# Output projection in steps of two heads, loads three steps ahead, six places per attention tile

## The chip, the core and the metric

The kernel runs on one core of one Trainium2 chip. Its time is the device time in microseconds; lower is better. TensorE does the matrix products, VectorE and ScalarE the work on elements, GpSimd fills constants, and SyncE issues nearly all DMA transfers. SyncE, like the other engines, works through its instructions in order: an instruction that waits holds up all behind it on that engine.

## What is computed

One decoder layer on two sequences of 512 tokens with 1024 features, in float32: attention with a sliding window of 128 and an output projection, cross products with a quantised context, and a quantised feed forward, each with a residual and a layer norm.

```python
def _L0_attn_ref(x, wq, wk, wv, wo):
    q = (x @ wq.T).reshape(B, N, N_Q, HD).transpose(0, 2, 1, 3)    # 32 heads of 128
    k = (x @ wk.T).reshape(B, N, N_KV, HD).transpose(0, 2, 1, 3)   # 8 heads
    v = (x @ wv.T).reshape(B, N, N_KV, HD).transpose(0, 2, 1, 3)
    o = _gqa_swa_attention(q, k, v, SLIDE)
    o = o.transpose(0, 2, 1, 3).reshape(B, N, N_Q * HD)
    return o @ wo.T
...
x = _layernorm(x + _L0_attn_ref(x, L0_attn_wq, L0_attn_wk, L0_attn_wv, L0_attn_wo), axis=-1)
x = _layernorm(x + _L0_xattn_ref(x, ctx_4096, ...), axis=-1)   # fake_quant(x) @ fake_quant(ctx)
x = _layernorm(x + _L0_ffn_ref(x, L0_ffn_w_gate, L0_ffn_w_up, L0_ffn_w_down), axis=-1)
```

The feed forward is silu(gate) * up with 2752 inner features, rounded to whole numbers, times w_down.

## The kernel before

**Products by Strassen's scheme.** Large products are cut into two by two blocks and done with seven block products instead of eight (`strassen`, L99; its matmuls are L109). The left factors need sums of weight blocks (`strassen_left`, L86, lines L92 to L95 on VectorE). A "piece" is one of the seven: four matmuls of 128x256 in float32, each of which the profile shows as two records.

**Attention** (`attention`, L181) goes over 16 groups, first the eight of sequence 0, then the eight of sequence 1. A group has four query heads and is done in four tiles of 128 tokens. In each tile stand, in program order: the scores (L294) with the softmax on VectorE and ScalarE (L301 to L316), pieces of the next group's projections (taken from `rest`), the transposes `pt` of the softmax's result (L322), its two copies `cur` and `both` (L328, L329), further pieces, and the weighing of the values (`weigh`, L341 and L342). A group has 22 pieces; four tiles of six take them all before the last tile's end, so that the last tile has four. Projection weights come through a pool of two buffers (`load_weight`, L203). At a group's end `keep` stores the attention output and its Strassen sums to a scratch tensor in DRAM (`kept`).

**Places.** At each call of `between` (three in a tile) `in_attention` (L903) lets a step of other work in. Three queues of such work exist. `behind` holds the context's quantisation and then the two output projections, one step a call. `aside` holds the cross products of sequence 0, one step a tile. `ahead` holds the sums of the output weights (`sum_output_weights`, 32 steps) and then of the gate and up weights (`sum_weights`, 42 steps): one step a tile while sequence 0 is in attention, two a tile after.

**Output projection** (`project_out`, L387). It runs one level of Strassen over the 32 heads: two halves `q` of the rows, seven products `k`, four steps `s` each, 56 steps. A step loads the left factor (`ol`, 256 KB) from `kept` and the right factor (`or`, 1024 KB) from the output weights or their sums, and does four matmuls of 128x512 (L434). The loads go one step ahead into two buffers. The projection of sequence 0 runs in the attention of sequence 1; that of sequence 1 starts in the last group, must wait for the last heads' `keep` for its steps with `s == LAST`, and runs on in the feed forward (`feed_forward`, L579), where `in_feed_forward` gives it four of the seven places of a unit.

**Order.** The framework places the instructions of each engine in an order of its own that follows data dependences and an estimate of durations; it is fixed when the kernel is built. So a VectorE operation may stand ahead of its place in the source, and waits there in order.

Of the kernel before, what the change touches and what calls it, by code (L numbers as in the profile page):

```python
# [9 lines left out]
F32 = mybir.dt.float32  # L10
# [8 lines left out]
P = 128  # L19
# [3 lines left out]
D = 1024  # L23
KC = D // P
NTT = NT // P
TPB = N // P
NQ = 32
NKV = 8
# [5 lines left out]
HALF = 512  # L34
KH = KC // 2
# [145 lines left out]
def attention(nc, tc, consts, xbuf, tpool, ps_p, ps_y, dram, kept, complete, between):  # L181
# [5 lines left out]
    with ExitStack() as ctx:  # L187
# [9 lines left out]
        STEPS = 6  # L197
# [3 lines left out]
        weights, lefts, right = {}, {}, {}  # L201
# [164 lines left out]
        for m, (b, g) in enumerate(groups):  # L366
            if m + 1 == NKV:
                x1 = load_x(1)
                right[1] = strassen_right(nc, tpool, x1, "t_1")
            rest = pieces(m + 1) if m + 1 < len(groups) else iter(())  # L370
            for i in range(TPB):
                s = scores(b, g, i)
                for _ in range(4):
                    next(rest, None)
                between(b, g, i)
                cur, both = transpose_p(b, g, i, s)
                between(b, g, i)
                for _ in range(STEPS - 4 if i < TPB - 1 else STEPS * TPB):
                    next(rest, None)
                weigh(b, g, i, cur, both)  # L380
                between(b, g, i)
            keep(b, g)
            if g == NKV - 1:
                complete.add(b)


def project_out(nc, b, xres, spaces, psum, kept, complete, wo_d, sums, x_d):  # L387

    respool, stream, work = spaces
    LAST = NKV // 2 - 1
    steps = [(q, k, s) for q in range(2) for k in (1, 6, 2, 7, 5, 4, 3) for s in range(LAST + 1)]

    steps[:8] = [(0, k, s) for k in (1, 6) for s in range(LAST)] + [(0, k, LAST) for k in (1, 6)]
    loaded = {}

    def load(n):
        if n >= len(steps):
            return  # L400
        q, k, s = steps[n]
        left = stream.tile([P, 2, 2, P], F32, tag="left", name=f"ol_{b}_{n}")
        nc.sync.dma_start(out=left, in_=kept[:, k - 1, ts(s, 2), :, ts(q, P)])
        right = stream.tile([P, 2, 2, HALF], F32, tag="right", name=f"or_{b}_{n}")
        src = wo_d[(0, 2, 3)[k - 1]] if k <= 3 else sums[:, k - 4]
        nc.sync.dma_start(out=right, in_=src[:, ts(s, 2)])
        loaded[n] = left, right

    while b and (b - 1, "tokens") not in complete:
        yield  # L410
    load(0)
    yield
    x = respool.tile([P, TPB, D], F32, tag="xres", name=f"xres{b}")
    for i in range(TPB):
        nc.sync.dma_start(out=x[:, i], in_=x_d[ts(b * TPB + i, P), :])
        xres[b * TPB + i] = x[:, i]
    for n, (q, k, s) in enumerate(steps):
        while n + 1 < len(steps) and steps[n + 1][2] == LAST and b not in complete:
            yield
        load(n + 1)  # L420
        left, right = loaded.pop(n)
        if s == 0:
            if k in (1, 6, 5):
                ps = psum.tile([P, HALF], F32, tag="p", name=f"y_{b}_{n}")
                if k == 1:
                    one = ps
                    p1, u2, u3 = (work.tile([P, HALF], F32, tag=f"y{j}", name=f"y{j}_{b}_{n}") for j in range(3))
                elif k == 6:
                    two = ps
                else:  # L430
                    three = ps
        ps = one if k in (1, 2) else three if k in (5, 3) else two
        for c in range(4):
            nc.tensor.matmul(  # L434
                ps, left[:, c // 2, c % 2], right[:, c // 2, c % 2],
                start=k in (1, 6, 5) and s == 0 and c == 0, stop=s == LAST and c == 3,
                skip_group_check=True,
            )
        if s == LAST:
            c11, c12, c21, c22 = (x[:, 2 * h + q, ts(e, HALF)] for h in range(2) for e in range(2))  # L440
            add = lambda out, in0, in1: nc.vector.tensor_tensor(out, in0, in1, ALU.add)
            if k == 1:
                nc.scalar.copy(p1, one)
            elif k == 6:
                add(u2, two, p1)
            elif k == 2:
                add(c11, one, c11)
            elif k == 7:
                add(u3, two, p1)
            elif k == 5:  # L450
                add(u3, three, u3)
                add(c22, u3, c22)
            elif k == 4:
                add(p1, two, p1)
                add(c21, p1, c21)
            else:
                add(u2, three, u2)
                add(c12, u2, c12)
                complete.add((b, q))
        yield  # L460
# [118 lines left out]
def feed_forward(nc, tc, ident, xres, spill, x2T, tpool, early, gate_up, wd_d, pools, stream, out, between, finish_between):  # L579

    wgu_d = gate_up[0]
    _, raw_pool, b_work, ps_p = pools
    with ExitStack() as ctx:
# [15 lines left out]
        acc, left, raw, halves, acts = {}, {}, {}, {}, {}  # L599
# [86 lines left out]
        def down(us, i, e):  # L686

            b, m = units[us[0]]
            t = b * TPB + i
            ps = ps_d.tile([P, HALF], F32, tag="d", name=f"d_{us[0]}_{i}_{e}")  # L690
            down_parts(ps, us, i, e, True, True)
            if m == 0:
                if e == 0:
                    acc[t] = accp.tile([P, D], F32, tag=f"acc{i}", name=f"acc{t}")
                nc.vector.tensor_copy(acc[t][:, ts(e, HALF)], ps)
            else:
                nc.vector.tensor_tensor(acc[t][:, ts(e, HALF)], ps, acc[t][:, ts(e, HALF)], ALU.add)  # L697
            if us[-1] % PER == NCHUNK and e == 1:
                x = stream.tile([P, 2, 2, HALF], F32, tag="right", name=f"fin_x_{t}").rearrange("p a b c -> p (a b c)")[:, :D]
                nc.sync.dma_start(out=x, in_=spill[t])  # L700
                ends.append((t, x, [acc[t]]))

# [87 lines left out]
def decoder_layer(ctx, tc, x, xT, ctx_kv, wq, wk, wv, wo, s1, z1, s2, z2, wgu, wgu_rest, wd, out):  # L790
    nc = tc.nc
    const = ctx.enter_context(tc.tile_pool(name="const", bufs=1))
    resid = ctx.enter_context(tc.tile_pool(name="resid", bufs=1))
    stream = ctx.enter_context(tc.tile_pool(name="stream", bufs=2))
    y_work = ctx.enter_context(tc.tile_pool(name="y_work", bufs=1))

    ident = const.tile([P, P], F32, tag="ident", name="ident")
# [74 lines left out]
    def sum_weights(pool):  # L872


        steps = [(m, k) for m in range(NCHUNK) for k in range(0, KH, 2)]

        def load(m, k):
            w = pool.tile([P, 2, 2, 2, P], F32, tag="w", name=f"raw_{m}_{k}")
            for h in range(2):
                for j in range(2):  # L880
                    c = j * KH + k
                    nc.sync.dma_start(out=w[:, h, j], in_=wgu[m, :, h, c : c + 2])
            return w

        ahead = load(*steps[0])
        for n, (m, k) in enumerate(steps):
            w = ahead
            if n + 1 < len(steps):
                ahead = load(*steps[n + 1])
            if k == 0:  # L890
                sums.append(scratch.tile([P, 4, KH, P], F32, tag=f"sums{m}", name=f"sums{m}"))
            a11, a12, a21, a22 = (w[:, h, j] for h in range(2) for j in range(2))
            s = pool.tile([P, 3, 2, P], F32, tag="s", name=f"sum_{m}_{k}")
            s1_, s2_, s4_ = (s[:, q] for q in range(3))
            tc.keep_in_program_order(nc.vector.tensor_tensor(s1_, a21, a22, ALU.add))
            nc.vector.tensor_tensor(s2_, s1_, a11, ALU.subtract)
            nc.vector.tensor_tensor(a21, a11, a21, ALU.subtract)
            nc.vector.tensor_tensor(s4_, a12, s2_, ALU.subtract)
            nc.sync.dma_start(out=sums[m][:, 0:3, k : k + 2], in_=s)
            nc.sync.dma_start(out=sums[m][:, 3, k : k + 2], in_=a21)  # L900
            yield

    def in_attention(b, g, i):  # L903
        calls[0] += 1
        if (b, g, i) == (0, 2, 0) and calls[0] % 3 == 1:
            behind.add(cross.context(0), 3)
        if (b, g, i) == (1, 0, 1) and calls[0] % 3 == 1:
            behind.add(output(0, ps_y))
            behind.add(output(1, pools[3]))
            aside.add(cross_tokens(0))  # L910
        behind.step()
        if calls[0] % 3 == 0:
            aside.step()
            if b and g == NKV - 1 and (0, "tokens") in complete and not early:
                prepare_feed_forward()
        if calls[0] % 3 == 0 and (b or g or i):
            ahead.step()
            if b:
                ahead.step()

    early = []

# [18 lines left out]
    def in_feed_forward(k):  # L941
        if k in (1, 5):
            aside.step()
        elif k != 3:
            behind.step()

    def finish_between():
        behind.drain()
# [55 lines left out]
```

## Time and profile before

| | us |
|---|---|
| median of 3 runs | 2029.87 |
| lowest and highest run | 2022.77, 2032.69 |
| the profiled execution | 2027.27 |
| its span, first to last instruction | 2024.8 |
| TensorE busy in it | 1962.9 (97%) |
| VectorE, ScalarE, GpSimd busy | 1185.1, 536.0, 14.2 |
| DMA, mean over the span | 213 GB/s, 430.6 MB |

The span has five parts: start (to about 27 us), the first attention (to about 480), the second attention with the first output projection (to about 1100), the feed forward with the second output projection (to about 1490), and the rest of the feed forward. TensorE's busy time counts a matmul that runs at half clock in full; the share of the clock that was granted stands beside it in the table by stretches. In a timeline, a bracket behind a row gives how long the engine stood idle before it and what ended that. "SPq" is SyncE's queue of DMA issues, and "to landing" is the time from issue to the last byte.

### The profile page before, as it was taken

The page shows a single profiled execution, that of the slowest core. Times are in us where ns is not written, and L with a number is a line of the kernel's source. Part 1 is how long each engine was busy: PE and PEld are TensorE (multiplying, and loading weights), DVE is VectorE, ACT ScalarE, POOL GpSimd, SP SyncE. Part 2 cuts the span into 40 slices and gives each one's busy share as a digit, 9 for nine tenths or more (in the row PEclk, how much of TensorE's full clock was granted, in tenths as well). Part 3 has the DMA queues.
Part 4 walks back from the last instruction along what each step waited for, and adds up shares of the span by engine and source line. Part 5 has one row for each costly group of instructions (what it writes and reads, how often), then busy time and mean ns, then how long its engine had stood idle before and what let it go on. Part 6 is the DMA issues. An engine that isn't in the chain of part 4 may idle for free.

```text
span 2024.8 us, 22067 instructions
## 1 busy us (share of the span) xinstructions
PE 1962.9 (97%) x8022; PEld 1445.1 (71%) x8032; DVE 1185.1 (59%) x2347; ACT 536.0 (26%) x1227; POOL 14.2 (1%) x34
## 2 busy tenths in 40 slices
PE   8999999999999999999999999999999999999995
PEld 6888878887655656666775666666678878888884
DVE  4666766675434355445854453633467688666666
ACT  1223332222111123122433221212133245222225
POOL 0000000000000000000000000000000000000000
PEclk9999999999999999999999999999999999999998
DMA  8355745557878887988537986667743435434421
GB/s 311 128 182 185 238 162 182 181 173 247 293 267 299 299 278 278 305 296 286 181 126 254 343 313 231 237 222 265 255 153 111 138 140 203 165 134 169 149 86 42
DMA packets 220012, 430.60 MB, mean 213 GB/s; under 512 B 16256, under 2 KB 150400, under 8 KB 200192
## 3 DMA queue, kind: packets, MB, share of 16 engines
q1 hardware_dynamic: 218752, 427.10, 60.4%
q10 hardware_dynamic: 1152, 2.10, 0.3%
q8 instruction: 63, 1.03, 0.2%
q14 instruction: 45, 0.37, 0.1%
HBM read 354.68 MB, written 74.45 MB: 212 GB/s over the span
## 4 chain that ended last, share of the span: by engine, by line
PE 79%; DMA 10%; DVE 6%; ACT 2%; issue 1%; SPq 1%; DVEq 0%; ACTq 0%
PE prod L109 43%; PE y L434 16%; PE d L683 8%; PE ps L294 4%; DMA or<-in_wo_dram 3%; DMA or<-wo_sums 3%; PE o L341 2%; DMA w<-in_wq_dram 2%; PE o L342 2%; PE m L551 1%; PE pt L322 1%; DMA xT<-in_xT_dram 1%; PE whole L676 1%; DMA w<-in_wv_dram 0%; DMA kept<-oS 0%
## 5 line engine op out<-in xcount | busy, mean ns | idle before, releaser
L434 PE MATMUL y<-or,ol 128*128 128x512 f32 x896 | 413.1, 604 | 24.0 <-DMA or<-in_wo_dram 12.2
L434 PEld LDWEIGHTS y<-or,ol 128*128 128x128 f32 x896 | 169.9, 193 | 203.9 <-issue 190.9
L109 PE MATMUL prod<-t,wgu 128*128 128x256 f32 x1312 | 302.2, 379 | 0.1
L109 PEld LDWEIGHTS prod<-t,wgu 128*128 128x128 f32 x1312 | 248.5, 190 | 45.4 <-issue 11.2
L109 PE MATMUL prod<-x2T,wgu 128*128 128x256 f32 x984 | 229.8, 379 | 1.0 <-DVE u_None L135 1.0
L109 PEld LDWEIGHTS prod<-x2T,wgu 128*128 128x128 f32 x984 | 186.6, 190 | 38.7 <-issue 12.4
L109 PE MATMUL prod<-xT,w 128*128 128x256 f32 x752 | 180.0, 380 | 1.3 <-ACT st L118 1.3
L109 PE MATMUL prod<-t,s 128*128 128x256 f32 x752 | 175.9, 379 | 0.0
L109 PE MATMUL prod<-t,w 128*128 128x256 f32 x752 | 175.2, 379 | 0.3 <-DVE st L121 0.3
L109 PEld LDWEIGHTS prod<-t,w 128*128 128x128 f32 x752 | 141.8, 190 | 21.9 <-issue 1.6
L109 PEld LDWEIGHTS prod<-t,s 128*128 128x128 f32 x752 | 141.0, 190 | 22.8 <-issue 3.3
L697 DVE TENSOR_TENSOR acc<-d,acc 128x512 f32<-128x512 f32 x152 | 104.7, 691 | 89.3 <-PE d L683 89.1
L109 PEld LDWEIGHTS prod<-xT,w 128*128 128x128 f32 x752 | 139.6, 190 | 24.2 <-issue 5.3
L683 PE MATMUL d<-hi,act 128*128 128x512 f32 x352 | 152.5, 433 | 2.3 <-DVE act L652 2.1
L683 PE MATMUL d<-lo,act 128*128 128x512 f32 x352 | 139.0, 395 | 0.0
L310 ACT ACTIVATE s<-s,top 128x128 f32<-128x128 f32 x256 | 99.7, 391 | 71.3 <-DVE top L307 71.2
L294 PE MATMUL ps<-kT,qT 128*128 128x256 f32 (+1 forms) x512 | 111.5, 353 | 0.0
L294 PEld LDWEIGHTS ps<-kT,qT 128*128 128x128 f32 x512 | 88.5, 190 | 30.7 <-issue 19.2
L302 DVE COPY_PREDICATED s<-mask_i,ps 128x512 f32<-128x512 int32 x64 | 46.7, 730 | 108.0 <-ACT s L301 103.3
L625 ACT CAST hi<-wd 128x1024 fp32r<-128x1024 f32 x44 | 46.0, 1046 | 226.5 <-PE d L683 115.9
L346 ACT COPY oT<-o 128x512 f32<-128x512 f32 x64 | 37.4, 585 | 216.8 <-PE o L342 109.1
L683 PEld LDWEIGHTS d<-hi,act 128*128 128x128 f32 x352 | 66.0, 187 | 39.7 <-DVE acc L697 20.4
(194 smaller groups left out, 2185.1 us busy)
## 6 DMA issues: line engine op xcount, KB each, us to landing
or<-wo_sums SPq DMA_DIRECT2D x64, 1024.0 KB, 6.3
or<-in_wo_dram SPq DMA_DIRECT2D x48, 1024.0 KB, 6.7
wgu<-sums SPq DMA_DIRECT2D x41, 1024.0 KB, 7.3
w<-in_wq_dram SPq DMA_DIRECT2D x64, 512.0 KB, 4.5
ol<-kept SPq DMA_DIRECT2D x112, 256.0 KB, 3.7
raw<-in_wgu_dram SPq DMA_DIRECT2D x168, 128.0 KB, 5.0
wd<-in_wd_dram SPq DMA_DIRECT2D x42, 512.0 KB, 3.8
wgu<-in_wgu_dram SPq DMA_DIRECT2D x41, 512.0 KB, 4.0
```

What stands on the lines that cost most here:

```text
L109: nc.tensor.matmul(ps, left[k - 1][:, c, :], right[k - 1][:, c, :], start=start and c == 0, stop=c == KH - 1, skip_group_check=True)
L294: nc.tensor.matmul(ps[:, h, :width], qT[b, g, h][:, ts(i, P)], kT[b, g][:, lo : lo + width], start=True, stop=True,)
L302: nc.vector.copy_predicated(s, mask_i.unsqueeze(1).to_broadcast([P, G, P]), ps[:, :, width - P : width])
L310: nc.scalar.activation(s[:, h, :], s[:, h, :], AF.Exp, bias=top[:, h : h + 1], scale=QSCALE, accum_out=total[:, h : h + 1],)
L322: nc.tensor.transpose(ps[:, h, :], s[:, h, :], ident)
L341: nc.tensor.matmul(ps, v[b, g][:, i - 1, :], both, start=True, stop=False)
L342: nc.tensor.matmul(ps, vd[b, g][:, i - 1, :], cur, start=False, stop=True)
L346: nc.scalar.copy(outputs[b, g, half][:, :, :, ts(place, P)], ps.rearrange("p (k j) t -> p k j t", k=2))
L434: nc.tensor.matmul(ps, left[:, c // 2, c % 2], right[:, c // 2, c % 2], start=k in (1, 6, 5) and s == 0 and c == 0, stop=s == LAST and c == 3,
L625: nc.scalar.copy(hi, raw[u])
L683: nc.tensor.matmul(ps, act[:, ts(i, P)], half[:, ts(e, HALF)], start=start and k == 0, stop=stop and k == len(parts) - 1)
L697: nc.vector.tensor_tensor(acc[t][:, ts(e, HALF)], ps, acc[t][:, ts(e, HALF)], ALU.add)
```

## The change

- The output projection's steps take one pair of matmuls (one `s` is one kv head with its two Strassen columns) instead of two: 112 steps for each sequence. Each loads half as much (`ol` 128 KB, `or` 512 KB). The pool `stream` has four buffers of half the size, and loads go three steps ahead.
- `between` is called six times in a tile: after each of the four pieces behind the scores, once between transposes and weighing (one piece before it and at most one after it), and after the weighing.
- `in_attention` counts six places. `behind` has a step at each, `context` one in six; `aside` one a tile. `ahead` has one a tile in both attentions, and one more at the third place of every odd tile of sequence 0.
- In the feed forward `behind` has a step in each of the seven places of a unit.
- `sum_weights` loads its tile with one DMA of 512 KB instead of four of 128 KB.

```diff
                 for _ in range(4):
                     next(rest, None)
+                    between(b, g, i)
+                cur, both = transpose_p(b, g, i, s)
+                next(rest, None)
                 between(b, g, i)
-                cur, both = transpose_p(b, g, i, s)
-                between(b, g, i)
-                for _ in range(STEPS - 4 if i < TPB - 1 else STEPS * TPB):
+                for _ in range(STEPS - 5 if i < TPB - 1 else STEPS * TPB):
                     next(rest, None)
                 weigh(b, g, i, cur, both)
                 between(b, g, i)
...
-    LAST = NKV // 2 - 1
+    LAST = NKV - 1
...
-    steps[:8] = [(0, k, s) for k in (1, 6) for s in range(LAST)] + [(0, k, LAST) for k in (1, 6)]
+    steps[: 2 * NKV] = [(0, k, s) for k in (1, 6) for s in range(LAST)] + [(0, k, LAST) for k in (1, 6)]
+    AHEAD = 3
...
-        left = stream.tile([P, 2, 2, P], F32, tag="left", name=f"ol_{b}_{n}")
-        nc.sync.dma_start(out=left, in_=kept[:, k - 1, ts(s, 2), :, ts(q, P)])
-        right = stream.tile([P, 2, 2, HALF], F32, tag="right", name=f"or_{b}_{n}")
+        left = stream.tile([P, 2, P], F32, tag="left", name=f"ol_{b}_{n}")
+        nc.sync.dma_start(out=left, in_=kept[:, k - 1, s, :, ts(q, P)])
+        right = stream.tile([P, 2, HALF], F32, tag="right", name=f"or_{b}_{n}")
         src = wo_d[(0, 2, 3)[k - 1]] if k <= 3 else sums[:, k - 4]
-        nc.sync.dma_start(out=right, in_=src[:, ts(s, 2)])
+        nc.sync.dma_start(out=right, in_=src[:, s])
...
-    load(0)
+    for n in range(AHEAD):
+        load(n)
...
-        while n + 1 < len(steps) and steps[n + 1][2] == LAST and b not in complete:
+        while n + AHEAD < len(steps) and steps[n + AHEAD][2] == LAST and b not in complete:
             yield
-        load(n + 1)
+        load(n + AHEAD)
...
-        for c in range(4):
+        for c in range(2):
             nc.tensor.matmul(
-                ps, left[:, c // 2, c % 2], right[:, c // 2, c % 2],
-                start=k in (1, 6, 5) and s == 0 and c == 0, stop=s == LAST and c == 3,
+                ps, left[:, c], right[:, c],
+                start=k in (1, 6, 5) and s == 0 and c == 0, stop=s == LAST and c == 1,
...
-    stream = ctx.enter_context(tc.tile_pool(name="stream", bufs=2))
+    stream = ctx.enter_context(tc.tile_pool(name="stream", bufs=4))
...
-            for h in range(2):
-                for j in range(2):
-                    c = j * KH + k
-                    nc.sync.dma_start(out=w[:, h, j], in_=wgu[m, :, h, c : c + 2])
+            src = wgu[m].rearrange("p h (j c) i -> p (h j) c i", j=2)
+            nc.sync.dma_start(out=w.rearrange("p h j c i -> p (h j) c i"), in_=src[:, :, k : k + 2])
...
-        if (b, g, i) == (0, 2, 0) and calls[0] % 3 == 1:
-            behind.add(cross.context(0), 3)
-        if (b, g, i) == (1, 0, 1) and calls[0] % 3 == 1:
+        place = calls[0] % 6
+        if (b, g, i, place) == (0, 2, 0, 1):
+            behind.add(cross.context(0), 6)
+        if (b, g, i, place) == (1, 0, 1, 1):
...
-        if calls[0] % 3 == 0:
+        if place == 0:
             aside.step()
...
-        if calls[0] % 3 == 0 and (b or g or i):
+        if (place == 0 and (b or g or i)) or (place == 3 and b == 0 and i % 2):
             ahead.step()
-            if b:
-                ahead.step()
...
         if k in (1, 5):
             aside.step()
-        elif k != 3:
-            behind.step()
+        behind.step()
```

More of the change, by code (lines that the diff above doesn't have):

```diff
@@ L698, in down @@
             if us[-1] % PER == NCHUNK and e == 1:
-                x = stream.tile([P, 2, 2, HALF], F32, tag="right", name=f"fin_x_{t}").rearrange("p a b c -> p (a b c)")[:, :D]
+                x = stream.tile([P, 2, HALF], F32, tag="right", name=f"fin_x_{t}").rearrange("p a b -> p (a b)")
                 nc.sync.dma_start(out=x, in_=spill[t])
```

## The prediction

> **What bounds the kernel now.** I read the busy time of the engines by stretch, then TensorE's waits, then the order of time around the longest of them. In the first table the columns are the stretch, its length, busy time and instruction count of PE, PEld, DVE, ACT and POOL, the granted clock, the DMA share and GB/s.
>
> ```profile
> 400.00:500.00 100.00, 99.72 (x445) 79.37 (x444) 68.59 (x145) 27.68 (x91) 0.52 (x1) 1.00 0.62 203
> 500.00:600.00 100.00, 95.69 (x332) 61.09 (x331) 41.63 (x91) 14.85 (x49) 0.53 (x1) 0.97 0.83 283
> 600.00:700.00 100.00, 94.20 (x331) 60.54 (x331) 43.25 (x95) 15.41 (x52) 0.52 (x1) 0.98 0.85 296
> 1800.00:1900.00 100.00, 100.00 (x453) 84.19 (x452) 63.97 (x109) 23.95 (x40) 0.00 (x0) 1.00 0.44 151
> ```
>
> TensorE is the bound: it is busy 1962.9 of 2024.8 us, and no edit removes a matmul. What can be had is its idle time and the time it runs below full clock. Both lie where the second batch's attention carries the output projection of the first (about 485 to 1160 us): busy 94 to 96%, clock 0.97 to 0.98, DMA share over 0.8.
>
> ```profile
> PE y L434 <- DMA or<-in_wo_dram: 12.2, 8, 3.1
> PE y L434 <- DMA or<-wo_sums: 8.0, 8, 3.1
> PE pt L322 <- DVE s L316: 5.2, 7, 1.4
> PE y L434 <- DMA ol<-kept: 3.8, 1, 3.8
> ```
>
> (us in total, times, longest.) The projection's matmuls wait 12.2 + 8.0 + 3.8 = 24.0 us for their loads; everything else that TensorE waits for inside the kernel is under 17 us. What follows such a wait is seen in the order of time:
>
> ```profile
> 549.42 3.60 PE L434 MATMUL y<-or,ol 128*128 128x512 f32 x8
> ...
> 558.70 6.58 PE L434 MATMUL y<-or,ol 128*128 128x512 f32 x8 [3.08 <-DMA or<-in_wo_dram]
> ...
> 611.70 5.37 PE L434 MATMUL y<-or,ol 128*128 128x512 f32 x8 [3.11 <-DMA or<-wo_sums]
> ...
> 1114.56 8.55 PE L434 MATMUL y<-or,ol 128*128 128x512 f32 x16 [3.80 <-DMA ol<-kept]
> ```
>
> Eight matmul records (one old step) take 3.60 us, but 6.58 and 5.37 after these waits, and 5.40 at 710.6 us after a wait of 2.03: 2.98 + 1.77 + 1.80, and 1.5 of the 8.55 (two steps, 7.05), make **8.1 us at half clock**. The Trainium skill ("TensorE: Matmul & The Clock Gate", HAM clock gate) says that the clock falls after an idle window of about 3.4 us. By that rule only the 3.80 us gap could cost clock, and removing the others would return 24.0 + 1.5. The rows show four falls, three of them after shorter gaps. I take the rows: **24.0 + 8.1 = 32.1 us** hang on these waits.
>
> Why the loads are late is seen in SyncE's queue before the wait at 558.70:
>
> ```profile
> 545.28 0.48 SPq L403 DMA_DIRECT2D ol<-kept  x1
> 547.76 1.97 SPq L882 DMA_DIRECT2D raw<-in_wgu_dram  x4
> ...
> 550.79 1.00 SPq L406 DMA_DIRECT2D or<-in_wo_dram  x1
> ```
>
> The step's right factor goes out 5.5 us after its left one, behind loads and stores of the gate and up sums, then needs 7.9 us to land.
>
> **The change, part by part.** Pitches from the timeline: a Strassen piece (8 records) 1.73 us, an old projection step 3.44, a new one 1.72, four transposes 0.44, scores 1.72, a weighing 1.72.
>
> *Two heads per step, loads three ahead, four buffers.* Same matmuls, same bytes, and 448 instead of 224 loads on SyncE. Old: a load goes out when the step before last ends; the tightest step leaves it T 0.44 + y 3.44 + 2 pieces 3.46 + weighing 1.72 = 9.1 us. New: three steps lie between, at least 3 pieces 5.19 + 3 steps 5.16 + 0.44 = 10.8 us, elsewhere 14 to 16. A right factor of 1024 KB lands in 6.3 to 6.7 us (median); 512 KB loads mostly in 3.6 to 5.5. So the load is ready with 4 us to spare even if SyncE is 2 us late. The Trainium skill ("DMA: Bandwidth & Descriptors", Bandwidth) speaks against this: batch transfers to 1 MiB or more. Rows: `or<-in_wo_dram` 1024 KB 6.7 us, `wo<-in_wo_dram` 512 KB 4.2. Taken as if nothing overlapped, two halves cost 8.4 instead of 6.7, 1.7 us for each of 112 steps = 190 us. But that fixed part overlaps: the DMA engines are at 0.73 to 0.87 in this stage, not full, and the small loads run two steps under TensorE's work. I take 0, keep the 190 as the bound. SyncE's issue: 12 loads x 0.33 to 0.5 us per 24.5 us tile (transposes at 507.15 and 531.70), some 8 us with all others; not full.
>
> *A third of the gate and up sums in the first attention; four raw loads as one.* A sums step moves 512 KB in and 512 KB out. The second attention's tiles go from two such steps to one: 1.05 MB less in 24.5 us, 43 of about 290 GB/s, and 3 loads fewer at about 0.5 us of issue for each step. This is what stood ahead of the late `or`. The first attention gets 16 more steps, one in each odd tile: 4 VectorE operations of 0.42 us, 27 us in all, where VectorE is 65 to 75% busy. Their place in the built order matters, as VectorE is in order and feeds `pt`. In tile 1 they come ahead of the last softmax multiply, but where VectorE now idles 1.53 us for a weight load (at 326.81), and strassen_left operations (0.6 each) move behind it: by the rows -0.6 to +0.5 us a tile. In tile 3 they fit a gap of 1.30 us between 355.95 and 357.25. Sum **0**, bounds -3 (most of the 4.7 us of `pt` waits there) and +12.
>
> *Six places per tile.* Tiles 0 to 2 have piece, step, piece between transposes and weighing: 1.73 + 1.72 + 1.73 = 5.2 us. Tile 3 of each group has no piece left there, and the cover falls from 3.44 to **1.72 us**. The two copies it has to hide (`cur`, `both`) take 1.5 us if VectorE is free. It is not always:
>
> ```profile
> 533.68 0.69 DVE L92 TENSOR_TENSOR s<-w 128x512 f32<-128x512 f32 x1 [4.79 <-DMA w<-in_wq_dram]
> ...
> 535.01 0.68 DVE L328 TENSOR_TENSOR cur<-pt,keep_cur 128x512 f32<-128x512 f32 x1
> ...
> 536.37 1.12 PE L341 MATMUL o<-both,v 128*128 128x512 f32 x2 [0.64 <-ACT both L329]
> ```
>
> In the built order of the changed kernel L92, which needs a weight load that can go out only when a late piece has freed its buffer, stands ahead of `cur` in five of the second attention's tiles 3. From the end of that piece to the weighing there are 1.72 + 1.73 + 1.72 + 0.44 + 1.72 = 7.3 us (old 9.1). Needed: landing 6.9 us (issued 526.73, used 533.68), L92 0.6, `cur` 0.7, `both` 0.6, 0.3 between: 9.1. That is a wait of 1.8 with today's traffic, near 0.5 with a landing of 5.6. I take 1.2 x 5 = **+6 us**, bounds 0 and 15.
>
> *End of attention.* After the last weighing the new order has half a step 0.86, piece 1.73, step 1.72, three pieces 5.19 = 9.5 us before the first step that needs the last group's late stores; old 1.72 + 6.9 = 8.6 before a 3.8 us wait. So about 3 us of wait stay. But then the new order goes to pieces of the second unit at once, whose weights (`wgu`) are issued behind the same stores 11 us after the weighing, where the old one still had two steps; and the next three left factors stand behind 1 MB of sums. About 2 us of new wait and 2 us of clock: 7, bounds 4 and 12. Other steps: 1.5 for what is left at lower DMA load, bounds 0 and 8.
>
> **Sum.** -32.1 + 7 + 6 + 1.5 + 0 = -17.6 us. Span 2024.8 - 17.6 = 2007.2. The profiled execution took 2027.27, 2.5 more than its span: 2009.7, so **2010 us**. The median of the runs shown, 2029.87, lies 2.6 above the profiled one and they spread over 10, so 2010 is 1.0% below the median. The feed forward's other parts, start and end stay: TensorE is at 98.7 to 100% there with the same work.
>
> **Rivals.**
> - *Everything hides* (20%). The w loads land in 5 us at the lower traffic, tile 3 doesn't wait, end of attention as now: -32.1 + 5 = 2000 us. For it: first-attention weight loads do land in 4 to 5 us. Against it: the load still goes out only when its buffer is free, and the 7.3 us stay.
> - *The wait moves* (13%). Three loads in flight lie ahead of the weight loads in the same queue; L92 and so the softmax and the weighing wait as much as the steps did. Five tiles 3 at 4 us and 10 us in others are 30 in place of 32.1: 2025 us, no change. For it: VectorE stood 4.6 to 5.9 us at L92 five times between 500 and 710 us. Against it: less DMA traffic there.
> - *Slower: VectorE blocked in the first attention* (10%). The sums there wait for their raw load, in order, ahead of the softmax, with no projection step to cover TensorE:
>
> ```profile
> DVE sum L895 <- DMA raw<-in_wgu_dram: 26.6, 9, 5.1
> ```
>
>   2.96 us each; in 16 odd tiles that is 47 us, 2010 + 47 = 2057. It decides from 1.9 us a tile (30 us, past 2040). Against it: the first attention's sums of the output weights (L864) show no wait for their load, and a load goes out two steps ahead, 13 us or more by the tiles' times.
> - That the change doesn't do what it says is excluded: the built order shows steps of two and pieces in turn.
>
> **How the numbers follow.** Forecast 57%, rivals 20, 13 and 10. The kernel's runs differ by 0.5%, about what can be told from no change: faster is below 2019.7, slower above 2040. Forecast (nearly all) and the first rival are faster, 77%; the third case and the forecast's upper end 13%; slower 10%. The range runs from the first rival, 2000 less 1, to the moved wait, 2026; slower stays out.
>
> **What would show it.** Right: y L434's waits (L437 now) fall from 24.0 to under 8 us, the clock in 500 to 800 us goes to 1.00 with no step at half speed, DMA below 260 GB/s there; `o L341 <- ACT both` grows from 0.6 to about 6; a wait near 1110 us stays. Wrong: `pt` waits in the first attention above 12 us, `or` waits at 10 or more, or SyncE's issue times well over 0.5 us each.

## The result and the profile after

| | before | changed |
|---|---|---|
| median, side by side on one chip (us) | 2026.86 | 2015.16 |
| lowest and highest | 2021.56, 2034.95 | 2010.19, 2022.99 |
| profiled execution (us) | 2027.27 | 2011.58 |
| its span (us) | 2024.8 | 2009.9 |
| TensorE busy (us) | 1962.9 | 1956.4 |

The changed kernel is faster: the ratio is 0.994, 95% interval 0.9921 to 0.9959. That is 0.6%, where 1.0% was forecast; the 2010 us of the forecast are 5 below the median, which lies in the range.

TensorE's waits in the changed kernel (us in total, times, longest) answer to those shown of before:

```profile
PE pt L322 <- DVE s L316: 11.6, 13, 2.0
PE o L341 <- ACT both L329: 6.4, 5, 1.6
...
PE prod L109 <- DMA wgu<-in_wgu_dram: 2.5, 1, 2.5
...
PE y L437 <- DMA or<-in_wo_dram: 1.3, 1, 1.3
PE y L437 <- DMA ol<-kept: 0.6, 1, 0.6
```

The projection's 24.0 us of waits are 1.9. But `pt` has gone from 5.2 to 11.6, and `o` from 0.6 to 6.4. The same stretches as before show where (columns as before):

```profile
200.00:300.00 100.00, 97.55 (x444) 78.34 (x443) 76.25 (x164) 32.03 (x92) 1.05 (x2) 0.98 0.73 242
...
500.00:600.00 100.00, 98.71 (x355) 64.55 (x354) 37.80 (x80) 16.33 (x51) 0.53 (x1) 1.00 0.82 265
600.00:700.00 100.00, 98.63 (x355) 64.66 (x354) 40.09 (x84) 17.39 (x58) 0.52 (x1) 1.00 0.84 268
1800.00:1900.00 100.00, 100.00 (x453) 84.16 (x452) 63.41 (x106) 21.80 (x36) 0.00 (x0) 1.00 0.42 147
```

In the second attention (500 to 700 us) TensorE is at full clock and busy 98.7% instead of 94 to 96%. The stretch 200 to 300 us, in the first attention, is now 97.55% busy at clock 0.98 with 242 GB/s; before it was

```profile
200.00:300.00 100.00, 99.20 (x453) 79.59 (x453) 74.47 (x154) 33.19 (x94) 1.05 (x2) 1.00 0.62 207
```

By the timeline, from the first transposes of one group to those of another, the first attention (groups 1 to 8) takes 374.1 us instead of 365.6, and the second (groups 8 to 15) 573.8 instead of 594.4. So **8.5 of 20.6 us were given back before the projection began**. The order of time on TensorE shows the costliest place there, then one of the five waits of `o`, then the end of attention:

```profile
225.86 0.63 PE L322 MATMUL pt<-ident,s 128*128 128x128 f32 x4 [1.97 <-DVE s L316]
226.33 1.50 PE L109 MATMUL prod<-t,s 128*128 128x256 f32 x4
227.62 3.15 PE L109 MATMUL prod<-xT,w 128*128 128x256 f32 x8
...
642.17 1.12 PE L341 MATMUL o<-both,v 128*128 128x512 f32 x2 [1.37 <-ACT both L329]
...
1102.21 1.95 PE L437 MATMUL y<-or,ol 128*128 128x512 f32 x4 [0.58 <-DMA ol<-kept]
1106.64 3.03 PE L109 MATMUL prod<-x2T,wgu 128*128 128x256 f32 x8 [2.47 <-DMA wgu<-in_wgu_dram]
```

A piece of eight records takes 1.89 us (1.88 to 1.89 in undisturbed rows). After the wait at 225.86 one takes 3.15, and four records before it 1.50: the clock is down for some 3.4 us, which loses 1.7. A second such fall follows the wait at 1106.64. Before there were four falls, costing 8.1 us. VectorE tells why `o` waits at 642.17:

```profile
168.44 0.69 DVE L92 TENSOR_TENSOR s<-w 128x512 f32<-128x512 f32 x1 [0.85 <-DMA w<-in_wq_dram]
...
170.45 0.17 DVE L315 RECIPROCAL inv<-total 128x4 f32<-128x4 f32 x1
...
170.85 0.68 DVE L316 TENSOR_TENSOR s<-s,inv 128x512 f32<-128x512 f32 x1
...
640.21 0.69 DVE L92 TENSOR_TENSOR s<-w 128x512 f32<-128x512 f32 x1 [2.81 <-DMA w<-in_wq_dram]
640.82 0.68 DVE L328 TENSOR_TENSOR cur<-pt,keep_cur 128x512 f32<-128x512 f32 x1
```

L92, the first sum of a left factor, stands in front and waits for its weight load; `cur` (L328) goes out the moment L92 is done. At 168.44 in the first attention it stands in the same way in front of the last steps of a softmax (L315, L316), and the transposes behind it wait 1.04 us (at 171.68). That wait is not new: before, the same transposes waited 1.43 us behind an L92 that stood 1.57 us. The waits that are new in the first attention stand elsewhere; the section on L92 shows them.

### The profile page after: what moved, and what is told of

Its sections match the earlier page's. It is cut to its first block, busy times and chain, and to the rows that moved or that the text cites. A ratio compares the mean times of both kernels' runs of the same rounds, so it can differ in the third digit from the quotient of the medians.

```text
span 2009.9 us, 22234 instructions
## 1 busy us (share of the span) xinstructions
PE 1956.4 (97%) x8032; PEld 1444.8 (72%) x8032; DVE 1178.3 (59%) x2347; ACT 527.7 (26%) x1221; POOL 14.2 (1%) x34
## 4 chain that ended last, share of the span: by engine, by line
PE 81%; DVE 8%; DMA 7%; issue 2%; ACT 2%; SPq 0%; DVEq 0%; ACTq 0%
PE prod L109 43%; PE y L437 18%; PE d L686 8%; DMA w<-in_wq_dram 4%; PE ps L294 4%; PE o L341 2%; PE o L342 2%; PE m L554 1%; PE pt L322 1%; DMA xT<-in_xT_dram 1%; PE whole L679 1%; DMA w<-in_wv_dram 1%; DVE s L316 0%; DVE s L93 0%; PE cs L525 0%
## 5 line engine op out<-in xcount | busy, mean ns | idle before, releaser
L437 PE MATMUL y<-or,ol 128*128 128x512 f32 x896 | 422.1, 592 | 1.8 <-DMA or<-in_wo_dram 1.3
L132 DVE TENSOR_TENSOR st<-prod,st 128x256 f32<-128x256 f32 x88 | 37.0, 420 | 128.9 <-PE prod L109 128.8
L294 PEld LDWEIGHTS ps<-kT,qT 128*128 128x128 f32 x512 | 87.9, 190 | 27.9 <-issue 16.6
```

The lines of the kernel that those rows point to most:

```text
L132: nc.vector.tensor_tensor(u3, two, p1, ALU.add)
L294: nc.tensor.matmul(ps[:, h, :width], qT[b, g, h][:, ts(i, P)], kT[b, g][:, lo : lo + width], start=True, stop=True,)
L437: nc.tensor.matmul(ps, left[:, c], right[:, c], start=k in (1, 6, 5) and s == 0 and c == 0, stop=s == LAST and c == 1, skip_group_check=True,)
```

## The experiments

Each kernel's ratio is to the kernel before, timed beside it on the same chip (its medians were 2026.24, 2028.13 and 2025.46 us on the three chips used); 95% intervals in brackets. A diff shows the lines that matter, and "..." stands for what is left out. Edits are against the changed kernel unless it says "before".

### Where the gain comes from

**A lead of one step with the small loads.**

```diff
-    AHEAD = 3
+    AHEAD = 1
-    stream = ctx.enter_context(tc.tile_pool(name="stream", bufs=4))
+    stream = ctx.enter_context(tc.tile_pool(name="stream", bufs=2))
```

> The changed kernel with two buffers and loads one step ahead, all else as changed (two heads, six places, sums moved). Theory (the lead of three steps removed the load waits): the projection's waits for or and ol come back, 10 us or more, with falls of the clock after them; time 2025 to 2035, that of the kernel before. Rival (the lighter DMA traffic and the even spread of the steps removed them, the lead is spare): waits stay under 5 us and the time at the changed kernel's 2015.

Measured: 2077.92 us, 1.0257 [1.0235, 1.028], over 40 us beyond what I expected. TensorE's waits in it:

```profile
PE y L437 <- DMA or<-wo_sums: 27.4, 33, 3.5
PE y L437 <- DMA or<-in_wo_dram: 23.9, 28, 2.2
```

Without the lead the projection waits 51.3 us, twice what it did before, at less traffic than before (234 GB/s against 265 between 481 and 1054 us). With a lead of one the half-sized step is a loss, since a step covers only half as much of the next load; the lead of three turns it into a gain. TensorE is also busy 16.8 us more than in the changed kernel. The last section comes back to this.

**The kernel before with the merged raw load only.** Before, with the one DMA of 512 KB in `sum_weights`:

```diff
-            for h in range(2):
-                for j in range(2):
-                    c = j * KH + k
-                    nc.sync.dma_start(out=w[:, h, j], in_=wgu[m, :, h, c : c + 2])
+            src = wgu[m].rearrange("p h (j c) i -> p (h j) c i", j=2)
+            nc.sync.dma_start(out=w.rearrange("p h j c i -> p (h j) c i"), in_=src[:, :, k : k + 2])
```

> The kernel before with one raw load of 512 KB for the gate and up sums instead of four of 128 KB, nothing else. Theory (the late right factor stands behind four raw issues of some 2 us in SyncE's queue): a good part of what the sums' part alone gave comes from this: load waits fall from 24.0 us to 12 to 18, time 2015 to 2022. Rival (it was the moved third, that is the traffic): waits stay at 20 to 24 us and the time at 2022 to 2030.

Measured: 2014.71 us, 0.9945 [0.9923, 0.9967], with no fall of the clock inside the kernel. The projection waits 6.2 + 4.6 + 3.6 = 14.4 us:

```profile
PE y L434 <- DMA or<-wo_sums: 6.2, 6, 1.5
...
PE y L434 <- DMA or<-in_wo_dram: 4.6, 6, 1.3
PE y L434 <- DMA ol<-kept: 3.6, 1, 3.6
```

Four lines of the diff give as much as the whole change. The traffic was not lowered (272 GB/s between 481 and 1054 us, 265 before), so 9.6 of the 24.0 us go without relief of the DMA engines. The likely reason is that one issue stands ahead of the right factor in SyncE's queue where four of 0.5 us stood; that one transfer of 512 KB may also land otherwise than four of 128 KB was not separated from it.

**The kernel before with the merged load and a third of the sums moved.** As the last one, and

```diff
-        if calls[0] % 3 == 0 and (b or g or i):
+        if (calls[0] % 3 == 0 and (b or g or i)) or (calls[0] % 3 == 1 and b == 0 and i % 2):
             ahead.step()
-            if b:
-                ahead.step()
```

> The kernel before with the sums' part alone: one more step in odd tiles of the first attention, one a tile in the second, one raw load instead of four; projection in steps of four heads, one ahead, three places. Theory: SyncE's queue and the traffic get lighter, so the 24.0 us of load waits fall, but not away: 10 to 18 us, and the first attention loses some 5; time within 8 us of before (2019 to 2030). Rival (traffic was the cause): waits under 5 us, time 2000 to 2010.

Measured: 2015.72 us, 0.995 [0.9931, 0.9969], below the 2019 to 2030 expected; the projection waits 10.6 us. Moving the third takes 3.8 us from those waits and nothing from the time.

**The two-head steps and the lead without the places or the merge.** Before, with steps of two heads, four buffers and loads three ahead; two half steps stand together at each of the three places.

```diff
...
-        behind.step()
+        for _ in range(2):
+            behind.step()
...
```

> The kernel before with the projection in steps of two heads, four buffers and loads three ahead, alone: three places as before with two half steps at each, sums and raw loads as before. Theory (the lead hides the loads whatever the traffic): load waits under 5 us, clock falls at most at the end of attention, weighing waits under 2 us since the cover stays 3.44, first attention as before; time 1995 to 2003, better than the changed kernel. Rival (places and traffic are needed with it): load waits of 8 us or more, time 2010 or more.

Measured: 2020.26 us, 0.9961 [0.9946, 0.9976]; waits 8.8 + 2.5 + 1.2 = 12.5 us for the loads, and 4.0 for `both`. I expected under 5. The lead in steps was there, but not in time.

**The same with the merged load.** It asks whether the four raw issues ate the lead. Against the last kernel:

```diff
...
-                    nc.sync.dma_start(out=w[:, h, j], in_=wgu[m, :, h, c : c + 2])
...
+            nc.sync.dma_start(out=w.rearrange("p h j c i -> p (h j) c i"), in_=src[:, :, k : k + 2])
```

> The kernel with the lead alone (three places, sums as before), and one raw load instead of four. Theory (SyncE's queue ate the lead: four raw issues and stores that wait stood ahead of three projection loads, which then went out together): load waits fall from 12.5 us to under 4, the two late weighings (4.0) stay, time 2002 to 2010. Rival (six places, with their even spacing of the loads, are what makes the lead work): load waits stay at 8 us or more, time 2012 or more.

Measured: 2015.62 us, 0.9953 [0.9935, 0.9971]; waits 9.6 + 5.1 + 1.9 = 16.6 us. They did not: without them the waits are no smaller. SyncE's queue of this kernel:

```profile
634.51 0.55 SPq L407 DMA_DIRECT2D or<-wo_sums  x1
...
645.74 1.29 SPq L407 DMA_DIRECT2D or<-wo_sums  x1
...
647.55 0.47 SPq L407 DMA_DIRECT2D or<-wo_sums  x1
...
648.54 0.62 SPq L407 DMA_DIRECT2D or<-wo_sums  x1
...
649.77 0.69 SPq L407 DMA_DIRECT2D or<-wo_sums  x1
```

The same queue in the changed kernel:

```profile
632.21 0.45 SPq L408 DMA_DIRECT2D or<-wo_sums  x1
...
635.67 0.46 SPq L408 DMA_DIRECT2D or<-wo_sums  x1
...
639.10 0.46 SPq L408 DMA_DIRECT2D or<-wo_sums  x1
...
641.26 0.46 SPq L408 DMA_DIRECT2D or<-wo_sums  x1
```

A load goes out when a step frees its buffer. Where two steps stand together, no right factor goes out for 11 us and then four within 4, and a step at 651.35 us waits 2.19 for one of them. With six places the loads go out 2 to 3.5 us apart, and the one longer gap (8.6 us, to 649.87) comes with three loads on their way. Worked out from the rows of issue and of matmul in the projection of sequence 0, a right factor has at least 8.8 us from issue to first use in the changed kernel (10.6 in nine cases of ten), but 5.1 (6.7) in this kernel, and 5.4 (6.5) before. In the median a right factor of 512 KB lands in 4.8 to 4.9 us in the changed kernel and 5.5 us in this one.

**Six places and the lead, with four raw loads and the sums as before.** The converse, in the changed kernel:

```diff
-            src = wgu[m].rearrange("p h (j c) i -> p (h j) c i", j=2)
-            nc.sync.dma_start(out=w.rearrange("p h j c i -> p (h j) c i"), in_=src[:, :, k : k + 2])
+            for h in range(2):
+                for j in range(2):
+                    c = j * KH + k
+                    nc.sync.dma_start(out=w[:, h, j], in_=wgu[m, :, h, c : c + 2])
...
-        if (place == 0 and (b or g or i)) or (place == 3 and b == 0 and i % 2):
+        if (place == 0 and (b or g or i)) or (place == 3 and b):
```

> The kernel with the sums moved back (1995 us), but with four raw loads instead of one: six places and three steps of lead with the traffic and queue of before. Theory (the queue eats the lead): load waits rise from 1.1 us to 5 to 12, time 2000 to 2012. Rival (six places and the lead are enough): waits under 3 us, time 1994 to 1999.

Measured: 1997.85 us, 0.9864 [0.9843, 0.9884]; TensorE's waits for the projection's loads are 2.9 us:

```profile
PE y L437 <- DMA or<-in_wo_dram: 2.2, 1, 2.2
...
PE y L437 <- DMA ol<-kept: 0.7, 1, 0.7
```

Lead and even places together are enough, with the full traffic and the four raw issues in the second attention. Neither alone is: three places leave 12.5 us, a lead of one 51.3. One thing comes with the six places and was not tested alone: a tile's two steps of sums, which stand together at three places, stand apart too (places 0 and 3).

### What takes part of it back

**The moved third put back into the second attention.** The merged load stays.

```diff
-        if (place == 0 and (b or g or i)) or (place == 3 and b == 0 and i % 2):
+        if (place == 0 and (b or g or i)) or (place == 3 and b):
```

> The changed kernel with the gate and up sums out of the first attention again: one step a tile there, two a tile in the second (places 0 and 3). Theory (the lead hides the traffic; the 16 extra steps cost the first attention 5.4 us of softmax waits and a clock fall): pt waits before 480 us fall from 10.1 to about 5, no clock fall there, the projection's load waits stay under 5 us, time 2006 to 2012. Rival (moving the sums is what freed the second attention): load waits of 10 us or more between 500 and 1000 us, DMA near 300 GB/s there, time 2020 or more.

Measured: 1995.27 us, 0.9851 [0.983, 0.9871], some 20 us below the changed kernel and more than I expected. The projection waits 1.1 us, `pt` 3.7, `o` not at all, and the first attention is back at 364.5 us. Its stretches (columns as before):

```profile
500.00:600.00 100.00, 100.00 (x359) 65.37 (x358) 44.08 (x98) 17.40 (x58) 0.53 (x1) 1.00 0.92 310
600.00:700.00 100.00, 100.00 (x363) 65.80 (x362) 49.29 (x108) 17.18 (x52) 1.05 (x2) 1.00 0.95 318
```

TensorE never stops where the DMA engines are busy 92 to 95% and move more than the kernel before did (283 and 296). Moving the sums away from this stage, which the forecast counted as relief, was not needed once lead and places were there, and cost 20 us. That `o` no longer waits was not foreseen: the built order has changed too, with L92 behind `cur` in tile 3.

**The last tile keeps one piece for behind the transposes.** This undoes the thin cover of 1.72 us.

```diff
-                for _ in range(4):
-                    next(rest, None)
+                for k in range(4):
+                    if k < 3 or i < TPB - 1:
+                        next(rest, None)
```

> The changed kernel, but the last tile of a group keeps one of its four pieces until after the transposes, so that the weighing has a piece and a step (3.45 us) ahead of it instead of a step (1.72). Theory (the weighing waits 1.05 to 1.6 us in five tiles because this cover is too short): o waits for both fall from 6.4 us to under 1, nothing else moves by over 2 us, time 2007 to 2011. Rival (the late weight load only moves to another wait, pt or the next product): o waits fall but pt or prod waits of the second attention grow by as much, time 2013 to 2017.

Measured: 1999.7 us, 0.9878 [0.9856, 0.99]. The 6.4 us of `o` are gone, as expected. But the gain is 15 us, since the first attention also fell from 374.1 to 368.0 us: an edit that touches one place lets the framework order VectorE's work anew everywhere. So these two kernels show that the waits can go, not which cause they had. Two others bear on `o`: with the merged load and a third of the sums moved in the kernel before, and with the lead and the merged load at three places, L92 stands ahead of `cur` in five tiles 3 of the second attention for 2.3 to 4.5 us, under a cover of 3.44 us, and `o` does not wait. With L92 ahead of `cur`, the size of the cover decides.

**L92 kept at its place in the source.** The moved third stays; only the order of the first operation of a left factor is fixed.

```diff
-    nc.vector.tensor_tensor(s1, a21, a22, ALU.add)
+    tc.keep_in_program_order(nc.vector.tensor_tensor(s1, a21, a22, ALU.add))
...
```

> The changed kernel with VectorE's weight sums (L92) held at their place in the source instead of hoisted to where the softmax and the weighing wait behind them. Theory (L92, waiting in order for a weight load, is what makes o and pt wait): o waits fall from 6.4 us to under 1, pt waits before 480 us from 10.3 to under 5, time 1998 to 2005. Rival (the 16 extra sums steps themselves, not L92, fill VectorE ahead of the softmax): pt waits stay at 8 us or more in the first attention, time 2006 to 2012.

Measured: 1995.14 us, 0.984 [0.9814, 0.9867]. L92 between 106 and 480 us, as a group (operation, shape, count | busy us, mean ns | idle time ahead of it and what ended it); first in the changed kernel,

```profile
L92 DVE TENSOR_TENSOR s<-w 128x512 f32<-128x512 f32 x21 | 14.5, 689 | 16.1 <-DMA w<-in_wq_dram 11.8 <-DMA w<-in_wv_dram 4.2
```

then with L92 in place, with one of TensorE's waits over the whole kernel:

```profile
L92 DVE TENSOR_TENSOR s<-w 128x512 f32<-128x512 f32 x22 | 14.9, 676 | 0.0
```

```profile
PE pt L322 <- DVE s L316: 1.3, 7, 0.2
```

The 16 extra steps run, at the same traffic (227 GB/s in that stretch, 222 in the changed kernel), and VectorE no longer stands at L92; `pt` waits 1.3 us in all and `o` does not wait. The rival, that the steps' own work delays the softmax, falls. But L92 alone is not the cause either: between 40 and 475 us it stands idle for its loads for 21.9 us in the changed kernel, 18.0 before and 15.6 with the third put back, and in these last two `pt` waits little.

What is new in the changed kernel is read from SyncE's queue. First the changed kernel, with the L92 that needs the last of these loads, then the kernel before at the same place:

```profile
308.46 0.35 SPq L210 DMA_DIRECT2D w<-in_wq_dram  x1
310.05 0.34 SPq L872 DMA_DIRECT2D wo_sums<-wo  x1
310.43 0.43 SPq L871 DMA_DIRECT2D wo_sums<-wo_sum  x1
310.91 0.51 SPq L210 DMA_DIRECT2D w<-in_wq_dram  x1
...
316.49 0.69 DVE L92 TENSOR_TENSOR s<-w 128x512 f32<-128x512 f32 x1 [2.39 <-DMA w<-in_wq_dram]
```

```profile
303.77 0.82 SPq L210 DMA_DIRECT2D w<-in_wq_dram  x2
```

Before, two weight loads go out together in tile 3. Now the added sums step is done there (L867 to L870 from 308.81 us on), and its two stores stand between the loads and wait for VectorE; the second load, which waits for nothing of its own, goes out some 2 us later, and L92 stands 2.39 us in tile 0 of the next group, where it did not wait before. In three more tiles 3 the second load goes out late in the same way, at 96.48, 148.75 and 363.49 us. The `pt` waits behind these four, at 106.47, 158.35, 321.34 and 373.63 us, are 3.4 us together. The longest wait, 1.97 us at 225.86, comes from another operation that stands for a load: VectorE stands 2.13 us at L498 for a context load that goes out at 211.66 us, behind four stores of `kept` (before at 204.86, ahead of three of them),

```profile
217.42 0.81 DVE L498 TENSOR_SCALAR raw<-raw,inv,par 128x1024 f32<-128x1024 f32 x1 [2.13 <-DMA raw<-in_ctx_dram]
```

and then works without a gap, through two steps of sums, up to the softmax. These five waits, 5.3 us, are nearly all by which `pt` has grown in the first attention (4.7 to 10.3).

With the third put back, with the piece held and with L92 in place, the loads of these four tiles go out in pairs again, and `pt` waits 3.7, 4.4 and 1.3 us before 480 us; with the lead of one they do not, and it waits 10.0. So each of these edits also changes SyncE's order. **What the traces show is the path: the added step's stores, waiting for VectorE, hold a load in SyncE's queue, and VectorE then waits in order for that load ahead of the softmax. Whether the last edit helps by L92's own place or by the new order of SyncE's queue was not separated.**

**Two edits at once.** First the third put back and the piece held, then the third put back and L92 in place:

```diff
-        if (place == 0 and (b or g or i)) or (place == 3 and b == 0 and i % 2):
+        if (place == 0 and (b or g or i)) or (place == 3 and b):
...
+                    if k < 3 or i < TPB - 1:
+                        next(rest, None)
```

> The changed kernel with the sums out of the first attention and a piece held back in a group's last tile, both together. Theory (both remove the same waits in the second attention, o for both, which are gone with either): 1990 to 1996, no more than 4 us under the kernel with the sums moved back. Rival (they add): 1976 to 1984.

```diff
-        if (place == 0 and (b or g or i)) or (place == 3 and b == 0 and i % 2):
+        if (place == 0 and (b or g or i)) or (place == 3 and b):
...
+    tc.keep_in_program_order(nc.vector.tensor_tensor(s1, a21, a22, ALU.add))
```

> The changed kernel with both: VectorE's weight sums held at their place and the gate and up sums out of the first attention. Theory (the two act in different stages: the pin's second attention took 563.8 us against 567.4, the moved sums' first attention 364.5 against 367.5): 1987 to 1992, below both (1995). Rival (what is left of waits is the same in both): 1993 to 1997.

Measured: 2000.91 us, 0.9867 [0.9839, 0.9894], and 1994.14 us, 0.9843 [0.9823, 0.9862], both outside what I expected. The first is worse than putting back the third alone: `pt` waits 7.4 us again, all in the first attention, and the clock fall at the end of attention lasts 6.8 us. Why that order brings these waits was not tested. The second closes a square of four (median, and `pt` waits in all):

| | third moved | third put back |
|---|---|---|
| L92 where the framework puts it | 2015.16, 11.6 | 1995.27, 3.7 |
| L92 in place | 1995.14, 1.3 | 1994.14, 0.7 |

As the rival of the second had it, the two edits remove the same cost. The three kernels at 1994 to 1995 us beat the kernel before by 1.5 to 1.6%, and the changed one by 1.0%.

## Why the prediction was right in direction and short in one term

The spans differ by 14.9 us where 17.6 were forecast; the medians by 11.7, as the profiled execution of the changed kernel lies 3.6 us below its median and that of the kernel before at its own. TensorE's idle and busy time give the sum term by term:

| term | forecast (us) | measured (us) |
|---|---|---|
| waits for the projection's loads | -24.0 + 3 + 1.5 | 24.0 to 1.9: -22.1 |
| half clock | -8.1 + 2 | 8.1 to 3.4: -4.7 |
| wait for `wgu` at the end of attention | +2 | +2.5 |
| weighing in tile 3 | +6 | 0.6 to 6.4: +5.8 |
| `pt` (first attention: 4.7 to 10.3) | 0 | 5.2 to 11.6: +6.4 |
| all else | 0 | -2.8 |
| sum | -17.6 | -14.9 |

- **Load waits and clock: right in kind and size.** The clock in 500 to 800 us is 1.00 and the projection's waits are under the 8 us named. The traffic at 500 to 700 us, 265 and 268 GB/s, is just above the 260 named. The reason given, a lead of "10.8 us, elsewhere 14 to 16", holds for nine loads of ten (10.6 measured); the least is 8.8. It holds only because the steps stand apart; the prediction took six places as a matter of cover behind the transposes and did not see that the lead hangs on them. Nor did the "9.1 us" of the old kernel's tightest step hold from issue to use (5.4 at least), as it left out the time in SyncE's queue. The relief "what stood ahead of the late `or`" was half right: fewer raw issues matter to the old structure (24.0 to 14.4 us), moving the third little (14.4 to 10.6, and nothing in time), and the new structure needs neither.
- **The rule of large transfers did not bind.** The Trainium skill ("DMA: Bandwidth & Descriptors", Bandwidth) advises batches of 1 MiB or more; the prediction's bound for halving them, 190 us with nothing overlapped, did not come, and the 0 that it took stands. With a lead of one, the halved step cost 51.3 us of waits, by its shorter cover.
- **The clock's idle window.** The prediction took the row of a fall after 2.03 us over the rule of the Trainium skill ("TensorE: Matmul & The Clock Gate", HAM clock gate), an idle window of about 3.4 us. The fall after 1.97 us at 225.86 agrees with that choice.
- **Weighing in tile 3: right.** "1.2 x 5" is 6.4 us in five tiles, by the mechanism named, L92 ahead of `cur` under the cover of 1.72 us.
- **End of attention: right.** Waits of 0.58 + 2.47 + 0.46 us near 1102 to 1110 and 1.7 of clock are 5.2; 7 was taken, 4 to 12 were the bounds.
- **The step that failed is "Sum 0" for the 16 sums in the first attention.** It took "-0.6 to +0.5 us a tile" and "a gap of 1.30 us" in tile 3 from VectorE alone, as if the loads came as before. The four operations do fit that gap; the step's two stores, for which the term has nothing, do not fit SyncE's queue. They stand ahead of a weight load in four tiles 3, L92 then waits 1.57 to 2.39 us ahead of the softmax of the next group, and a context load comes late in one more place. The stage grew by 8.5 us, within the bounds of -3 and +12: 5.6 of `pt`, 1.7 of a fall of the clock that no term had, and the rest in small parts.
- **The rival that the wait moves came in part.** `pt` and `o` together wait 12.2 us more, over half of the 22.1 that the loads gave back. But the new `pt` waits lie in the first attention, where what stands ahead of the weight loads is not the projection's loads, as that rival had it, but the stores of the sums.
- **The slower rival did not come.** It had VectorE stand at the sums' raw load. Those sums stood 0.2 us ahead of L896 to L899 together between 106 and 480 us; the operation that stood was L92.

## What to carry to other kernels

A prefetch depth counted in steps is worth only the time that lies between the steps: spread them evenly before adding buffers, and check the time from issue to use in the queue of issues, where several small issues ahead of a late load may be the cheapest thing to remove. On an engine that works in order, look for operations that the scheduler has moved ahead and that wait for a load; work added to a stage with idle time on that engine can cost through them, not through its own duration. Look at the transfers of added work too: a store that waits for its data holds the loads issued behind it. When such an order is built by a scheduler, an edit in one place shifts waits in others, on the issuing engine too, so compare the orders of both kernels before a faster edit is taken for the cause.

## What the runs showed of the hardware

**A wait costs more than its idle time.** The kernel with the lead of one has 61 waits for loads, two falls of the clock like the changed kernel, and 16.8 us more of TensorE's busy time. If all of that belongs to these waits, it is some 0.3 us a wait. Its order of time on TensorE around one of them:

```profile
649.37 1.03 PE L109 MATMUL prod<-xT,w 128*128 128x256 f32 x4
651.60 1.95 PE L437 MATMUL y<-or,ol 128*128 128x512 f32 x4 [1.20 <-DMA or<-wo_sums]
```

The step after the wait takes 1.95 us instead of 1.88, and the four records ahead of it 1.03, 0.16 more than half of a piece's pitch of 1.73.

**The length of a wait does not decide the clock.** It fell after waits of 1.97 us (changed kernel) and 2.03 (before), but only twice in the kernel with 61 waits up to 3.5 us, and not at all after a wait of 3.60 us in the kernel before with the merged load only:

```profile
1100.17 6.28 PE L434 MATMUL y<-or,ol 128*128 128x512 f32 x14 [3.60 <-DMA ol<-kept]
```

The 14 records take 6.28 us, 0.45 each as in an undisturbed step (3.60 for eight), and the granted clock is 1.00. What decides it stays open.

**Nearly full DMA engines did no harm.** 318 GB/s at a share of 0.95 lay beside a TensorE that was busy 100% of the stretch, while with two steps at a place (the lead with the merged load) it waited and was busy 98.5 and 97.8% of the same stretches, at 317 and 313 GB/s.
